# An attention and expert-mixture kernel: expert slots padded to quarters of a tile instead of halves

## Chip, cores and metric

The kernel runs on one core of a Trainium2 chip. The metric is the device time in microseconds (us) of one execution. A core has five engines with queues of their own: TensorE (PE, with its weight loads listed as PEld), VectorE (DVE), ScalarE (ACT), GpSimd (POOL) and SyncE (SP), which here only issues DMAs.

## What is computed

Input x has 2 x 2048 tokens of 256 numbers; all is float32. After a layernorm, two branches are added to x: a linear attention with Chebyshev features and prefix sums, and a mixture of experts in which each token goes to one of 8 experts, beside one shared expert.

```python
xn = _layernorm(x)
# attention: 16 heads of 16, clipped q and k, Chebyshev orders 0..10, cumsum over the tokens
kv_prefix = jnp.cumsum(Tk * v[:, :, :, None, :], axis=2)
ks_prefix = jnp.cumsum(Tk.sum(axis=-1), axis=2)
num = (Tq * kv_prefix * beta).sum(axis=3)
den = (Tq.sum(axis=-1) * ks_prefix * beta).sum(axis=3)
attn = (num / (den + 1e-7)) @ W_out.T
# experts
xf = _layernorm(xn, ln_w, ln_b).reshape(-1, 256)
logits = xf @ router_w
top_idx, top_score = argmax(logits), sigmoid(max(logits))
for e in range(8):                     # g, u: 256 x 512, d: 512 x 256
    xe = xf * where(top_idx == e, top_score, 0.0)
    routed += (silu(xe @ g[e]) * (xe @ u[e])) @ d[e]
shared = (silu(xf @ sh_gate) * (xf @ sh_up)) @ sh_down
out = x + attn + xn + routed + shared
```

## The kernel before

The 4096 tokens are 8 chunks of 512, or 32 tiles of 128. The kernel never runs its stages one after the other. It declares operations (`op`: engine, expected cost, what it reads and writes, a priority, buffers to allocate), and a planner (`Plan.order`) places them on the engines by a model of time: of the operations that are ready, and whose buffers are free, each engine takes the one with the lowest priority number. The planned order is then the program; on the chip each engine runs its own list in that order and waits on semaphores. Priorities put the front first (0), routing (2), scattering (4), expert fetches and small expert work (6), attention (10 and up), the experts' gate and up products (30 and up), and the shared expert last (50 and up), so the shared expert fills PE where nothing else is ready.

**Front.** For each chunk `stat` (L421, L422) takes mean and variance, `roots` (L432 to L456) the inverse roots with one Newton step (L440 to L445; the square root is ACT's, L435), and `front` normalizes (L480, L484), transposes on PE (L505), and evicts to xfT, the experts' input, on ACT (L508) or DVE (L510), and to xnT, the attention's. For chunk 0 the first half of xfT is evicted by ACT, the second by DVE. At the very start ACT issues five small DMAs (L385, L387: ln weights and router) and then runs one square root on a dummy (L390), which loads ACT's table. L462 transposes the ratio that later chunks' xnT need. xnT and most xfT are spilled to DRAM (L566, L571) and loaded again when wanted (L832).

**Routing** (`route`, L675 to L824) is DVE work with two small products: it picks the expert of each token and a slot for it. With padding to whole tiles, 8 experts need up to 39 tiles of 128 slots. The kernel pads to halves: NFULL = 28 tiles hold one expert each, and 15 half tiles (NHALF) follow, two to a tile, so NJ = 36 tiles and NI = 43 sets of expert weights. `odd` counts for each expert the tiles begun, `full` the tiles of which more than a half is used (L711 to L719, a comparison with the multiples of 128, then of 128 plus 64). From them come first and last tile of each expert, the slot of each token (L736 to L762), the expert of each tile (`expert_i`, L768 to L774) and the tables `take_i`, `give_i`, `slot_s` (L781 to L824).

**Experts** (`expert`). For each tile SP reads the expert's number (L1087) and fetches its weights from DRAM, gate and up (L1089) and down (L1095), 512 KiB each, into places of the pool `w_p`. POOL gathers the tokens (L1100); PE transposes them (L1108); ACT scales them (L1111); PE takes the gate and up products (L1118), ACT and DVE silu and product (L1124, L1126), PE transposes (L1131), ACT or DVE copy (L1133, L1134), PE takes the down product (L1139), and after a copy (L1142, L1143) POOL scatters to y_dram (L1146). In a half tile each product is two matmuls with 64 stationary columns each, one for each expert. `w_p` has 8 places of 1024 columns; ten more come from the two attention buffers T when the attention's elementwise work is over. Four of the eight serve the routing tables first.

**Attention** (`attend`): q, k, v products (L907), features on ACT and DVE, prefix sums by scans on DVE (L974), sums over heads on PE (L937, L950, L955: 32 stationary columns each, four groups of columns side by side), denominators (L1018, L1031), output product (L1045).

**Shared expert** (`shared`): gate and up (L845) and down (L862) of each chunk; its xfT, except for chunks 0 to 2, is loaded again into one of four xfT places. A chunk's load waits for the chunk before, and chunks 6 and 7 for the up products of an expert tile near the end (`hold`).

**End**: when all tiles are scattered, y is read back in eight loads (L1169) into xnT and xfT places, added (L1178) and written out (L1182).

The line that sets the order of the tiles before, and the hold:

```python
tiles = sorted(range(NJ), key=lambda j: j if j < NFULL else (j - NFULL + 0.5) * NFULL / n2 - 0.25)
gate, hold = [], {NC - 2: ups[-9], NC - 1: ups[-2]}
```

Of the kernel before, what the change touches and what calls it, by code (L numbers as in the profile page):

```python
# [11 lines left out]
F32 = mybir.dt.float32  # L12
# [24 lines left out]
HF = P // 2  # L37
NFULL = NTT - NE // 2
NHALF = 2 * NTT + NE - 1 - 2 * NFULL
NJ = NFULL + (NHALF + 1) // 2  # L40
NI = NFULL + NHALF
# [214 lines left out]
def kernel(  # L256
# [78 lines left out]
    wide = const.tile([P, 4618], F32, name="wide")  # L335
# [43 lines left out]
    for c in range(NC):  # L379
        if c == 0:  # L380
            for t in range(NT):
# [6 lines left out]
               w=["ln"], nbytes=64 * KiB, prio=-89)  # L388

            op("ACT", 0.2, lambda: A.activation(nu[:, 0, 0:1], ones[:, 0:1], AF.Sqrt), w=["root"], prio=-88.5,  # L390
# [21 lines left out]
    xfTs, xnTs, spilled, fronts, begun = {}, {}, [], [], []  # L412
# [3 lines left out]
    def stat(c):  # L416
        for t in range(NT):
            i = c * NT + t

            def f(c=c, t=t, i=i):  # L420
                V.bn_stats(stats[:, i, :], X[c][:, t, :])  # L421
                V.bn_aggr(mv[:, i, :], stats[:, i, :])  # L422
            op("DVE", 0.58, f, r=[("X", c, t)], w=[("mv", i)], prio=FRONT + 0.1 * c - 0.15)

    def roots(cs):
# [12 lines left out]
        def h():  # L438
# [4 lines left out]
            V.tensor_tensor(u_, u_, v_, ALU.mult)  # L443
            V.tensor_scalar(u_, u_, -0.5, 1.5, ALU.mult, ALU.add)
            V.tensor_tensor(r_, r_, u_, ALU.mult)  # L445
        op("DVE", 1.0, h, r=[("ve", a), ("rs", a)], w=[("r", a // NT + k) for k in range(len(cs))], prio=p)
# [21 lines left out]
    def front(c):  # L468
# [31 lines left out]
        for k in range(KD):  # L500
            bk = Buf(bank_p, f"tr_{c}_{k}")

            def f(bk=bk, k=k):
# [9 lines left out]
            op(*on[k if c == 0 else 0], r=[bk, "ln"], w=[(xfT, k)],  # L513
               prio=p if c else -2.0, alt=on[1:] if c else [])
            if c:
# [117 lines left out]
    def route():  # L633
# [10 lines left out]
        top, idx, lim, pos, tok1, score, hi = (t2(n) for n in ("top", "idx", "lim", "pos", "to", "sc", "hi"))  # L644
# [12 lines left out]

        tile_of = wide[:, : NTT * NJ].rearrange("p (t j) -> p t j", t=NTT)
# [9 lines left out]
        def f():  # L668
# [3 lines left out]
            V.tensor_scalar(lim, iota[:, :NTT], float(P), None, ALU.mult)  # L672
# [33 lines left out]
        def f():  # L706
            for e in range(NE // 2, NE):
                V.tensor_tensor_scan(incl[:, e, :], ones[:, :NTT], tot[:, e, :], 0.0, ALU.mult, ALU.add)

            n_e = incl[:, :, NTT - 1 : NTT].to_broadcast([P, NE, NTT])  # L710
            V.tensor_tensor(gt, n_e, lim.unsqueeze(1).to_broadcast([P, NE, NTT]), ALU.is_gt)  # L711
        op("DVE", 1.3, f, r=["tot", "iota"], w=["gt"], prio=R)

        def f():
            n_e = incl[:, :, NTT - 1 : NTT].to_broadcast([P, NE, NTT])
            V.tensor_reduce(odd, gt, AX.X, ALU.add)
            V.tensor_scalar(lim, lim, float(HF), None, ALU.add)
            V.tensor_tensor(gt, n_e, lim.unsqueeze(1).to_broadcast([P, NE, NTT]), ALU.is_gt)
            V.tensor_reduce(full, gt, AX.X, ALU.add)  # L719
        op("DVE", 1.3, f, r=["gt", "iota"], w=["full"], prio=R)  # L720

        def f():
# [6 lines left out]
            V.tensor_tensor(lft, odd, full, ALU.add)  # L729
            V.scalar_tensor_tensor(lft, wh, -2.0, lft, ALU.mult, ALU.add)  # L730
# [3 lines left out]
        def f():  # L734
# [3 lines left out]
            V.tensor_scalar(lft, lft, float(HF), float(NFULL * P), ALU.mult, ALU.add)  # L738
# [317 lines left out]
    for g in range(KD):  # L1056
# [4 lines left out]
                             zt_p.add([b.t[:, 5120 : 5120 + D]])))  # L1061
    for i, (q, n) in enumerate(((zt_p, D), (sl_p, FF), (hm_p, FF), (yt_p, D))):
# [8 lines left out]
    def expert(n, j):  # L1071
# [3 lines left out]
        if j >= NFULL:  # L1075
            h = NFULL + 2 * (j - NFULL)
            parts = [(h, slice(0, HF)), (h + 1, slice(HF, P))] if h + 1 < NI else [(h, slice(0, P))]
# [7 lines left out]
        for i, ((h, _), (wg, wu, wd)) in enumerate(zip(parts, sets)):  # L1085
            def f(h=h, wg=wg, wu=wu):
                ev.append(nc.values_load(expert_i[0:1, h : h + 1], engines=[SP], min_val=0, max_val=NE - 1))  # L1087
# [137 lines left out]
```

## Time and profile before

| what | value |
|---|---|
| median of 3 runs | 582.14 us (581.93 to 582.86) |
| profiled execution, its own time | 582.48 us |
| its span (first to last instruction) | 580.7 us |
| instructions | 7507 |
| DMA traffic | 110.87 MB, mean 191 GB/s |
| expert gate / up / down loads | 43 each, 512 KiB each |
| L1118 on PE, all forms | 344 instructions listed |
| L1139 on PE, all forms | 344 instructions listed |
| first expert product (L1118) | 139.0 us |
| last load of expert weights issued | 511.69 us |
| last down product (L1139) ends | 544.35 us |
| first y load issued | 548.73 us |
| last matmul ends | 577.06 us |

How to read it: the profile lists for each group of instructions the line of the kernel, engine, operation and shape, the number of instructions, and times in us (means in ns). Each float32 matmul is two matmul instructions on PE. The chain of waits follows what ended last backward to what released it; a row is start, duration, engine and line, and the number of instructions. A stage's row gives start and end, length, busy time of PE, PEld, DVE, ACT and POOL with instruction counts, the granted PE clock, the DMA share and GB/s. The row of a wait gives who waited for whom, the total, how often, and the longest.

### The profile page before, as it was taken

What the parts mean: (1) busy time and instruction counts of PE and PEld (TensorE: products, weight loads), DVE (VectorE), ACT (ScalarE), POOL (GpSimd) and SP (SyncE); (2) the same over time, 40 slices, a digit from 0 to 9 for tenths busy, and PEclk for the clock granted to TensorE, in tenths of its full rate; (3) what the DMA queues carried; (4) which work ended last, traced back from release to release, by engine and by line L of the source; (5) the groups of instructions that cost most, each with busy time, mean ns of one, the idle gap of its engine ahead of it and who ended that gap; (6) DMA issues with size and microseconds to landing.
All of it is one profiled execution on the core that took longest, in us unless ns stands there. A gap on an engine that the chain in (4) does not pass through costs nothing. (4 is left out here: it accounts for less than half of the span.)

```text
span 580.7 us, 7507 instructions
## 1 busy us (share of the span) xinstructions
PE 567.2 (98%) x2439; PEld 312.0 (54%) x2439; DVE 488.4 (84%) x797; ACT 242.6 (42%) x478; POOL 98.5 (17%) x116
## 2 busy tenths in 40 slices
PE   4999999999999999999999999999999999999997
PEld 2446464675554644547464545545465457555565
DVE  6989899999999999999999889999999999433263
ACT  3878872105433553353354454336335432122100
POOL 3201000011211112201303211221121132302100
PEclk9999999999999999999999999999999999999999
DMA  8956570434266825735736672884666386990195
GB/s 270 302 174 215 218 256 34 145 133 126 73 206 216 259 83 175 244 116 165 227 134 209 200 225 70 242 256 156 201 214 199 116 246 228 332 357 28 41 372 176
DMA packets 73142, 110.87 MB, mean 191 GB/s; under 512 B 5425, under 2 KB 44623, under 8 KB 73104
## 3 DMA queue, kind: packets, MB, share of 16 engines
q1 hardware_dynamic: 68144, 99.63, 52.3%
q0 software_dynamic: 4112, 10.77, 5.8%
q8 instruction: 19, 0.31, 0.2%
q10 hardware_dynamic: 848, 0.01, 0.1%
q14 instruction: 19, 0.16, 0.1%
HBM read 91.50 MB, written 19.41 MB: 191 GB/s over the span
## 5 line engine op out<-in xcount | busy, mean ns | idle before, releaser
L1118 PE MATMUL bank<-big,wide 128*128 128x512 f32 (+1 forms) x320 | 122.3, 599 | 0.0
L1146 POOL DMA_INDIRECT y_dram<-wide,give_i x34 | 42.5, 1249 | 308.2 <-ACT wide L1142 159.3
L907 PE MATMUL bank<-xnT,w_in 128*128 128x512 f32 x192 | 87.4, 595 | 0.0
L974 DVE TENSOR_TENSOR_SCAN tv<-ones,carry,tv 128x512 f32<-128x512 f32 x60 | 76.6, 1276 | 1.1
L1118 PEld LDWEIGHTS bank<-big,wide 128*128 128x128 f32 (+1 forms) x320 | 44.7, 171 | 56.4 <-issue 54.5
L845 PE MATMUL bank<-xfT,sg 128*128 128x512 f32 x128 | 62.4, 610 | 0.1
L1139 PE MATMUL bank<-big,wide 128*128 128x256 f32 (+1 forms) x312 | 61.8, 386 | 0.0
L845 PE MATMUL bank<-xfT,su 128*128 128x512 f32 x128 | 60.7, 597 | 0.0
L862 PE MATMUL bank<-sd,hT 128*128 128x256 f32 x256 | 57.6, 380 | 0.0
L907 PEld LDWEIGHTS bank<-xnT,w_in 128*128 128x128 f32 x192 | 35.4, 190 | 38.1 <-issue 34.1
L1139 PEld LDWEIGHTS bank<-big,wide 128*128 128x128 f32 (+1 forms) x312 | 44.0, 171 | 20.5 <-issue 9.7
L862 PEld LDWEIGHTS bank<-sd,hT 128*128 128x128 f32 x256 | 48.0, 190 | 10.0 <-issue 3.0
L1100 POOL DMA_INDIRECT wide<-z_dram,take_i x33 | 38.4, 1163 | 78.5 <-DVE wide L823 68.7
L851 ACT ACTIVATE hT<-bank 128x512 f32<-128x512 f32 x32 | 19.1, 596 | 75.7 <-PE bank L845 74.9
L1124 ACT ACTIVATE wide<-bank,slot_s 128x512 f32<-128x512 f32 x35 | 24.1, 687 | 61.1 <-PE bank L1118 61.1
L994 DVE TENSOR_TENSOR o<-o,tv 128x512 f32<-128x512 f32 x64 | 44.2, 691 | 1.7
L1126 DVE SCALAR_TENSOR_TENSOR wide<-bank,slot_s,wide 128x512 f32<-128x512 f32 x35 | 26.2, 748 | 19.0 <-PE bank L1118 17.1
L1111 ACT ACTIVATE wide<-bank,lnb,lnw 128x128 f32<-128x128 f32 x72 | 29.1, 457 | 25.0 <-PE bank L1108 25.0
L929 DVE SCALAR_TENSOR_TENSOR T<-T 128x1024 f32<-128x1024 f32 x32 | 38.3, 1216 | 0.0
L845 PEld LDWEIGHTS bank<-xfT,sg 128*128 128x128 f32 x128 | 23.5, 194 | 26.8 <-issue 23.3
L845 PEld LDWEIGHTS bank<-xfT,su 128*128 128x128 f32 x128 | 23.2, 190 | 25.5 <-issue 24.5
L853 DVE TENSOR_TENSOR hT<-hT,bank 128x512 f32<-128x512 f32 x32 | 21.9, 684 | 16.1 <-PE bank L845 15.0
(209 smaller groups left out, 804.7 us busy)
## 6 DMA issues: line engine op xcount, KB each, us to landing
big<-in_gate_w SPq DMA_DIRECT2D x40, 512.0 KB
big<-in_up_w SPq DMA_DIRECT2D x40, 512.0 KB
big<-in_down_w SPq DMA_DIRECT2D x39, 512.0 KB
z_dram<-big SPq DMA_DIRECT2D x8, 512.0 KB
X<-in_x SPq DMA_DIRECT2D x7, 512.0 KB
xn_dram<-xnT SPq DMA_DIRECT2D x7, 512.0 KB
xnT<-xn_dram SPq DMA_DIRECT2D x7, 512.0 KB
out<-X SPq DMA_DIRECT2D x7, 512.0 KB
```

The lines of the kernel that those rows point to most:

```text
L845: T_.matmul(b.t, wt[:, k, ts(f, P)], vx(k), start=(k == 0), stop=(k == KD - 1))
L862: T_.matmul(po.t[:, ts(i, D)], hT[f].t[:, ts(tp * 2 + i, P)], sd[:, f, :], start=(f == 0), stop=(f == KF - 1))
L907: T_.matmul(pm.t, w_in[:, k, ds(i * D + g * P, P)], xnT.t[:, ts(k, CH)], start=(k == 0), stop=(k == KD - 1))
L929: op("DVE", 1.27, lambda i=i, j=j, q=part: V.scalar_tensor_tensor(q[i](), q[j](), off[i], q[1](), ALU.subtract, ALU.mult), r=[(T, j)] + X2 ...
L974: o_ = op("DVE", 1.25, lambda b=b, i=i, g=g: V.tensor_tensor_scan(b.t, ones[:, 0:1].to_broadcast([P, CH]), b.t, 0.0 if opening else old[:, ...
L994: op("DVE", 0.66, lambda o=o, b=b: V.tensor_tensor(o(), o(), b.t, ALU.add), r=[b, ok], w=[ok], prio=p)
L1100: op("POOL", 1.28, lambda: G.indirect_dma_start(out=zt.t, out_offset=None, in_=z_dram, in_offset=bass.IndirectOffsetOnAxis(ap=take_i[:, j ...
L1111: op("ACT", 0.46, lambda k=k: A.activation(xT.t[:, ts(k, P)], pz.t[:, ts(k, P)], AF.Identity, bias=lnb[:, k : k + 1], scale=lnw[:, k : k + ...
L1118: T_.matmul(b.t[n, :], xT.t[:, ds(k * P + n.start, n.stop - n.start)], wt.t[:, ts(k, FF)], start=(k == 0), stop=(k == KD - 1), skip_group_ ...
L1126: op("DVE", 0.75, lambda: V.scalar_tensor_tensor(sl.t, pu.t, sc(), sl.t, ALU.mult, ALU.mult), r=[pu, zt, sl], w=[sl], prio=EXQ)
L1139: T_.matmul(py.t[n, :D], hmT.t[:, ds(i * P + n.start, n.stop - n.start)], wd.t[:, ts(i, D)], start=(i == 0), stop=(i == KF - 1), skip_grou ...
L1146: y_ins.append(G.indirect_dma_start(out=y_dram, out_offset=bass.IndirectOffsetOnAxis(ap=give_i[:, j : j + 1], axis=0), in_=yt.t, in_offset ...
```

## The change

- Slots are padded to quarters of a tile (32 slots). NFULL = 26 tiles of one expert, NPART = 31 quarters, four to a tile, in 8 more tiles (the last has three): NJ = 34 tiles, NI = 57 weight sets. A mixed tile has an expert in each quarter of its columns, so each of its products is four matmuls with 32 stationary columns.
- Routing counts quarters: one comparison of each expert's count with 128 multiples of 32 (`over`, in memory that the ratio rows used, hence its wait on the last xn_dram write), one sum for `odd` (quarters begun) and one over every fourth for `full`.
- The weights are fetched one at a time: all gates of a tile, then all ups, then all downs, each fetch with its own place.
- Two of the four xfT places go to `w_p` when the front's spills are issued (`V_`).
- The mixed tiles come first and then after each 3.7 whole tiles or so (before: after each 3.5); chunks 6 and 7 of the shared expert wait for the 14th and 4th last up products (before: 9th and 2nd).
- At the start: ACT's dummy square root comes ahead of its DMAs; the statistics of later chunks wait until chunk 0's second eviction has been issued (`evicted`); the Newton step has four DVE operations instead of five.

```diff
-HF = P // 2
-NFULL = NTT - NE // 2
-NHALF = 2 * NTT + NE - 1 - 2 * NFULL
-NJ = NFULL + (NHALF + 1) // 2
-NI = NFULL + NHALF
+NFULL = NTT - 3 * NE // 4
+NPART = 4 * NTT + NE - 1 - 4 * NFULL
+NJ = NFULL + (NPART + 3) // 4
+NI = NFULL + NPART
...
-               w=["ln"], nbytes=64 * KiB, prio=-89)
-            op("ACT", 0.2, lambda: A.activation(nu[:, 0, 0:1], ones[:, 0:1], AF.Sqrt), w=["root"], prio=-88.5,
+               w=["ln"], nbytes=64 * KiB, prio=-88.5)
+            op("ACT", 0.2, lambda: A.activation(nu[:, 0, 0:1], ones[:, 0:1], AF.Sqrt), w=["root"], prio=-89,
...
-            op("DVE", 0.58, f, r=[("X", c, t)], w=[("mv", i)], prio=FRONT + 0.1 * c - 0.15)
+            op("DVE", 0.58, f, r=[("X", c, t)], w=[("mv", i)], prio=FRONT + 0.1 * c - 0.15, after=evicted)
...
-            V.tensor_tensor(u_, u_, v_, ALU.mult)
-            V.tensor_scalar(u_, u_, -0.5, 1.5, ALU.mult, ALU.add)
-            V.tensor_tensor(r_, r_, u_, ALU.mult)
+            V.scalar_tensor_tensor(u_, u_, -0.5, v_, ALU.mult, ALU.mult)
+            V.scalar_tensor_tensor(r_, u_, 1.5, r_, ALU.add, ALU.mult)
...
-            op(*on[k if c == 0 else 0], r=[bk, "ln"], w=[(xfT, k)],
+            o = op(*on[k if c == 0 else 0], r=[bk, "ln"], w=[(xfT, k)],
                prio=p if c else -2.0, alt=on[1:] if c else [])
+            if c == 0:
+                evicted[:] = [o]
...
-            n_e = incl[:, :, NTT - 1 : NTT].to_broadcast([P, NE, NTT])
-            V.tensor_tensor(gt, n_e, lim.unsqueeze(1).to_broadcast([P, NE, NTT]), ALU.is_gt)
...
-            V.tensor_reduce(odd, gt, AX.X, ALU.add)
-            V.tensor_scalar(lim, lim, float(HF), None, ALU.add)
-            V.tensor_tensor(gt, n_e, lim.unsqueeze(1).to_broadcast([P, NE, NTT]), ALU.is_gt)
-            V.tensor_reduce(full, gt, AX.X, ALU.add)
+            V.tensor_tensor(
+                over, incl[:, :, NTT - 1 : NTT].to_broadcast([P, NE, 4 * NTT]),
+                quart.unsqueeze(1).to_broadcast([P, NE, 4 * NTT]), ALU.is_gt,
+            )
+        op("DVE", 1.3, f, r=["incl", "iota", ("xn_dram", NC - 1)], w=["gt"], prio=R)
...
+            V.tensor_reduce(odd, over, AX.X, ALU.add)
+            V.tensor_reduce(full, over.rearrange("p e (t q) -> p e t q", q=4)[:, :, :, 3], AX.X, ALU.add)
...
-            V.tensor_tensor(lft, odd, full, ALU.add)
-            V.scalar_tensor_tensor(lft, wh, -2.0, lft, ALU.mult, ALU.add)
+            V.scalar_tensor_tensor(lft, wh, -4.0, odd, ALU.mult, ALU.add)
...
+    for i in range(2):
+        b = Buf(xfT_p, f"V_{i}")
+        b.users = 1
+        op("SP", 0.01, lambda: None, alloc=[b], prio=ROUTE, after=list(spilled),
+           grow=lambda b=b: w_p.add([b.t]))
...
-            h = NFULL + 2 * (j - NFULL)
-            parts = [(h, slice(0, HF)), (h + 1, slice(HF, P))] if h + 1 < NI else [(h, slice(0, P))]
+            h = NFULL + 4 * (j - NFULL)
+            m = min(4, NI - h)
+            parts = [(h + i, slice(i * QD, (i + 1) * QD if i < m - 1 else P)) for i in range(m)]
...
-            fetch = op("SP", 1.3, f, r=["experts"] + [("z_dram", n) for n in range(NC)], w=[wg, wu], alloc=[wg, wu],
-                       nbytes=KiB * KiB, prio=EXQ + e, after=downs[-1:])
...
+        for n, src, cost in ((0, gate_w, 0.85), (1, up_w, 0.45), (2, down_w, 0.45)):
+            for i, (h, _) in enumerate(parts):
+                def f(h=h, i=i, n=n, src=src, b=sets[i][n]):
+                    if n == 0:
+                        ev.append(nc.values_load(expert_i[0:1, h : h + 1], engines=[SP], min_val=0, max_val=NE - 1))
+                    S_.dma_start(out=b.t.rearrange("p (k f) -> p k f", k=KF if n == 2 else KD),
+                                 in_=src[ds(ev[i], 1)].rearrange("o (k p) f -> p (o k) f", p=P))
+                downs.append(op("SP", cost, f, r=["experts"] + [("z_dram", n) for n in range(NC)], w=[sets[i][n]],
+                                alloc=[sets[i][n]], nbytes=512 * KiB, prio=EXQ + e, after=downs[-1:]))
...
-    tiles = sorted(range(NJ), key=lambda j: j if j < NFULL else (j - NFULL + 0.5) * NFULL / n2 - 0.25)
+    tiles = sorted(range(NJ), key=lambda j: j if j < NFULL else 3.7 * (j - NFULL) - 0.5)
...
-    gate, hold = [], {NC - 2: ups[-9], NC - 1: ups[-2]}
+    gate, hold = [], {NC - 2: ups[-14], NC - 1: ups[-4]}
```

## The prediction

> **What bounds the kernel now.** I read the busy times and the 40 slices first:
>
> ```profile
> PE 567.2 (98%) x2439; PEld 312.0 (54%) x2439; DVE 488.4 (84%) x797; ACT 242.6 (42%) x478; POOL 98.5 (17%) x116
> PE   4999999999999999999999999999999999999997
> DVE  6989899999999999999999889999999999433263
> ```
>
> TensorE works from 8.21 us (its first matmul) to 577.06 us (its last). Its clock was granted at full in every slice, so time is saved only by giving PE less work, or lost by making it wait. Second, DVE is 9 in nearly every slice until about 493 us, where the last attention chunk's elementwise work ends; after that it is half idle. PE therefore fills the gaps of a DVE-paced attention with expert tiles, and what is left with the shared expert.
>
> Then the chain of waits, which from 320 us on is almost only PE; its rows give the price of each kind of PE work:
>
> ```profile
> 355.01 0.86 PE psq L937 x8
> 357.79 1.00 PE psk L937 x8
> ...
> 443.37 1.87 PE bank L1118 x8
> ...
> 489.61 1.73 PE bank L1139 x8
> ...
> 504.38 1.88 PE bank L1139 x16
> ...
> 511.60 0.22 PE bank L1108 x2
> 511.82 0.44 PE bank L1131 x4
> 512.26 1.72 PE bank L1118 x4
> ```
>
> L1118 with 4 instructions is the gate (or up) product of a whole tile; with 8, of a half tile (two experts, 64 columns each): 1.87 against 1.72. So two column halves run side by side, at 0.15 for the change of form. L937 is the same with 32 columns, four groups side by side: 8 instructions of 512 elements take 0.86, or 1.00 where the form is entered. That is the shape the quarter tiles will have.
>
> Last the waits of the SP queue and two stages at the end:
>
> ```profile
> SPq L1089 <- PE bank L1139: 95.3, 20, 13.5
> SPq L1089 <- PE bank L1118: 56.3, 27, 10.8
> SPq L1095 <- PE bank L1118: 54.9, 19, 12.5
> ...
> 490.00:512.00 22.00, 22.00 (x91) 11.69 (x90) 11.22 (x19) 4.79 (x12) 6.55 (x6) 1.00 0.90 295
> 512.00:548.00 36.00, 36.00 (x130) 21.89 (x129) 11.13 (x18) 7.45 (x16) 5.93 (x6) 1.00 0.33 118
> ```
>
> SP, which fetches the experts' weights, mostly waits for PE to give a weight buffer back: buffers, not bandwidth, hold the fetch. From 140 to 490 us the DMA share is 0.59 at 186 GB/s; in the dense part after 497 us slices reach 350 to 425 GB/s, about 375, so one 512 KiB load costs 0.524 MB / 375 = 1.4 us at best.
>
> **The change, part by part.**
>
> *Two tiles fewer.* NJ goes from 36 to 34. A whole tile on PE is 0.22 + 1.72 + 1.72 + 0.44 + 1.73 = 5.83; two are **-11.7 us**, all on the engine that sets the end.
>
> *Quarters for halves.* Seven half tiles paid 0.15 three times (gate, up, down): 7 x 0.45 = 3.2. Eight quarter tiles, if L937 is the pattern, pay 0.14 to 0.15 three times: 8 x 0.45 = 3.6. I take **+0.5**. For the down product (four groups that move 256 elements) there is no row. The low bound is the same price; the high bound comes from L1018 (32 columns, 128 elements), whose 8 instructions take 0.36, 0.18 a wave of four where half of 0.215 (an eighth of 1.72) would be 0.11: 0.07 x 8 waves x 8 tiles = +4.5. L1118's and L937's forms are nearer in length, so I stay at the low end.
>
> Here a rule of the Trainium skill speaks against the change. The row first: L937's four groups took 0.86 to 1.00 where one full-width product takes 0.86, so 3.4 to 4 times one group's work. "TensorE: Matmul & The Clock Gate", section "Measured speedup vs the span model", gives three column tiles of 32 as 2.38 times, 79% of ideal. By that, as an estimate, the 5.17 us of products in a quarter tile become 6.5, eight tiles cost +11, and the saving is gone: about 581. The measured row decides, and I do not use the page's figure.
>
> *Weights.* Each quarter tile fetches four experts: 57 sets instead of 43, or 171 loads instead of 129, +22 MB; SP issues 42 more at 0.37 us each, which its long waits hide. At 1.4 us a load, 171 loads are 240 of the 430 us between 107 us (first fetch) and the last tile, so bandwidth is enough. What decides is the buffers. Before: 8 loads issued by 140 us, 104 between 140 and 490, 17 after; with 8 buffers one load stays in its buffer for 350 x 8 / 104 = 27 us. After: 10 buffers (two freed xfT places join). To be as far at 490 us as before, 171 x 112 / 129 = 148 loads must be out; less the 10 of the first fill, 138 in 350 us, so a stay of 25.4 us. This is 6% less than 27. Gate, up and down are now fetched singly, gates of all four experts first, which helps: before, gate and up were planned as a pair that needed two free buffers at once. The cover for a late weight is shared-expert work: of its 165 us (256 L845 instructions at 0.43, 256 L862 at 0.215), some 42 us were spent between 140 and 490 as filler (56 and 80 instructions in the trace), and the new holds (the 14th and 4th last tile instead of the 9th and 2nd) release chunks 6 and 7 earlier. If the stay remains 27 us: 350 x 10 / 27 + 10 = 140 loads by 490, 31 left, 31 x 1.4 = 43 us, last weights at 533 and, with some 8 us for the last tile, last expert product at 541. Before it was 544.35. So even an unchanged stay is just good enough. I take 1.5 us for extra PE waits at quarter tiles (before: PE's waits after the start came to 1.5 in all) with bounds 0 and 15.
>
> *After the last expert tile.* Two xfT places fewer mean three y loads in flight at the end, where five were issued between 548.73 and 551.4. A load takes 552.64 - 548.73 = 3.9 and its addition 1.22, so three buffers pass eight chunks in about 14 us; the additions in the trace are spread to 570.85 anyhow, behind PE. Nothing, as long as the shared filler (33 us of PE after 544.35) covers it; without that cover this tail of some 30 us (8.4 MB at 375 GB/s is 22.4, plus 4.4 from the last product to the first y load, plus latency and last addition) ends the kernel by itself.
>
> *Routing.* Removed: L711, L716, L717, L718, L719 (0.43 + 0.42 + 0.17 + 0.43 + 0.42 = 1.87) and L729 (0.17). Added: a comparison and a sum over 1024 elements, 1.2 each by L781 (1184 elements, 1.37) and L788 (1152, 1.35), a sum over 256 at 0.42, and about 0.25 for 57 instead of 43 experts in L768 and L772. Table work shrinks by 36 to 34 columns: -0.4. Net about +0.6 us of DVE. It lies before 127 us, while PE has shared work (L845 runs back to back from 96 to 106); behind it queue the first gather and expert tile at 138.9. The added wait for xn_dram's last write costs nothing: it was issued at 79.3, the comparison runs at about 94. I take 0, bounds 0 and +0.6.
>
> *The start.* The rows, of ACT, DVE and PE in order of time:
>
> ```profile
> 4.98 1.28 ACT L390 ACT_TABLE_LOAD   x1 [4.98 <-DMA lnw<-in_ln_w]
> 6.38 0.19 ACT L435 ACTIVATE rs<-ve 128x8 f32<-128x8 f32 x1
> 10.46 3.94 PE L845 MATMUL bank<-xfT,sg 128*128 128x512 f32 x4
> 11.72 0.81 DVE L510 TENSOR_SCALAR xfT<-bank,lnw,lnb 128x512 f32<-128x512 f32 x1
> ```
>
> The square root's table now loads before ACT's five DMA issues. The variances are ready at 5.82, so the root starts 0.5 earlier; one DVE operation fewer saves 0.2. The second eviction (L510) moves ahead of chunk 1's four statistics, and PE's second pair of L845 no longer stands for 2 us. But L462 waits for chunk 1's ratio at 16.58, which comes only 0.5 to 0.7 earlier, so most of the 2 us is handed on to that wait. The moved DMAs (lnw, lnb, router) are issued some 1.5 us later; lnw took 2.65 to land, so about 5 us, and is first used at 9.65: covered. Past that cover SP suffers: L392, and behind it sg, su and chunk 1, waited for such a landing (3.48). If it does again, chunk 1 is 1.5 later. I take **-0.8**, bounds -2 and +1.
>
> *Sum*, against the profiled execution's own 582.48 (span 580.7, 1.8 around it): 582.48 - 11.7 + 0.5 + 1.5 - 0.8 = 572.0. The median of the runs shown is 0.34 lower, which is inside the working: **572**.
>
> **Rivals.**
>
> *The tail shows (still faster).* Weights come a little late, PE spends the shared filler before the last expert tile, and the tail of 30 to 33 us ends the kernel. By the sums above with a last product between 544 and 548: span 575 to 580, so 576 to 581. For it: the final stage has 18 buffers' worth of loads and the quarter tiles reach into it (the last one is the last tile). Against: chunks 6 and 7 can be held for the tail by the plan.
>
> *Slower: the buffers.* One mechanism: a quarter tile needs 4 gates at once and 12 loads in all through 10 buffers, and the stay grows. At 30 us only 350 x 10 / 30 + 10 = 127 loads are out by 490; 44 left, 62 us, last product at 560, plus 32: span 592, **594**. It decides from a stay of 28 us: 135 loads out, 36 left, 50 us, last product at 548.7, plus 32 is the old 580.7. For it: loads per tile grow by 5.03 / 3.58 = 1.40 and buffers by 1.25, and a half tile's first gate already lay 40 us (fetched at 193.56, used at 229.56, released after 233). Against: PE's only waits for data now are 1.5 us, and much of a stay is PE doing attention.
>
> *Not what it says.* The four groups run one after the other: three more times 5.17 us, eight times, +124: 696. L937 is against it.
>
> **How the numbers follow.** Forecast 0.45 (own range 568 to 575.5), visible tail 0.24, within no change 0.05, slower by buffers 0.25, serial groups 0.01. No change means within 0.2%, 581.0 to 583.3, about what a measurement of this kernel can tell. So faster 0.69, same 0.05, slower 0.26. The predicted time is the likeliest case's. The range 567 to 588 takes in the start's and the down product's bounds, the tail and half of the slower case.
>
> **What would show it.** Right: PE busy near 556 us and still 9 in every slice; L1118 of the 32-column form at 16 instructions in some 1.9 us; PE's waits for weights under 3 us; last expert product before 541. Wrong: PE rows waiting for gate weights, or a PE that ends 5 us or more before the span does; L1139 of 32 columns above 2.2 us a tile; L505 at the start not before 8 us. Weights that lie 28 us or longer in the buffers would make the forecast wrong at its root.

## The result, and the profile after

The changed kernel takes **591.49 us** (median of 4 runs, 589.52 to 591.74) against 582.26 (median of 4, 581.93 to 582.86): a ratio of 1.015, 95% interval 1.0127 to 1.0173. It is slower by 9.2 us, where 572 was forecast. The profiled execution took 589.52 us, with a span of 587.6. Line numbers from here on are those of the changed kernel unless a run of the kernel before is meant: L504 is the front's transpose (before L505), L849 and L866 the shared expert (L845, L862), L911 the attention's q, k, v (L907), L1107 the gather (L1100), L1115 its transpose (L1108), L1125 gate and up (L1118), L1146 down (L1139), L1153 the scatter (L1146).

First the page of the changed kernel, busy times and slices:

```profile
PE 561.6 (96%) x2651; PEld 303.1 (52%) x2651; DVE 484.2 (82%) x784; ACT 242.4 (41%) x474; POOL 97.5 (17%) x112
PE   1999999999999999899899998999999999999997
DVE  3889999999999999899979988999989998831253
```

PE's busy time has fallen by 5.6 us, half of what was expected, and its line now has holes: a 1 in the first slice (before a 4), and eights between 235 and 367 us. DVE's line dips in the same stretch, so it has not taken over as the bound. The span grew although the work shrank, so the loss is in waiting. The waits of PE (who waited for whom, total, times, longest) name the place:

```profile
PE bank L504 <- DVE big L479: 13.0, 1, 13.0
PE bank L1115 <- DMA wide<-z_dram,take_i: 8.2, 7, 2.8
PE bank L911 <- ACT wide L1140: 0.7, 1, 0.7
```

The kernel before had these:

```profile
PE bank L505 <- DVE big L480: 8.2, 1, 8.2
PE bank L1108 <- DMA wide<-z_dram,take_i: 1.3, 1, 1.3
```

No row of the changed kernel has a weight's load in it. Two rows have grown: the first matmul, and the transposes of gathered tokens, 1.3 us before and 8.2 now.

**The start.** ACT's rows in order of time (start, duration, engine, line, operation, and in brackets the idle time before it):

```profile
0.82 1.28 ACT L389 ACT_TABLE_LOAD   x1 [0.82 <-PEq L1218]
2.11 0.20 ACT L389 ACTIVATE nu<-ones 128x1 f32<-128x1 f32 x1
2.99 0.41 ACTq L384 DMA_DIRECT2D lnw<-in_ln_w  x1
3.96 0.33 ACTq L384 DMA_DIRECT2D lnb<-in_ln_b  x1
4.51 0.33 ACTq L384 DMA_DIRECT2D lnw<-in_ln_w  x1
6.80 0.33 ACTq L384 DMA_DIRECT2D lnb<-in_ln_b  x1
10.89 0.39 ACTq L386 DMA_DIRECT2D rw<-in_router_w  x1
11.32 0.21 ACT L435 ACTIVATE rs<-ve 128x8 f32<-128x8 f32 x1 [9.01 <-DMA lnw<-in_ln_w]
```

The last two of the five small DMAs before, and two of SP's loads in the changed kernel:

```profile
2.23 0.46 ACTq L385 DMA_DIRECT2D lnb<-in_ln_b  x1
4.56 0.39 ACTq L387 DMA_DIRECT2D rw<-in_router_w  x1
```

```profile
2.68 0.43 SPq L391 DMA_DIRECT2D sg<-in_sh_gate  x1
...
3.67 0.47 SPq L396 DMA_DIRECT2D X<-in_x  x1
```

The table is loaded at 2.1 us, as meant. But the five small DMAs, of which the first four had gone by 2.7 us before, now go at 2.99, 3.96, 4.51, 6.80 and 10.89, and the root that the first transposes need (L435) stands behind them on ACT: 11.32 instead of 6.38. Each row of a DMA in the trace carries the semaphore that it raises. SP's and ACT's DMAs use the same eight, 100 to 107, and take them in turn by planned order; one that is given a semaphore already in use has a wait on it. Before, ACT's four norm loads were among the first eight and waited for nothing. Now SP has taken all eight: the second lnb load waits on 104, which the shared expert's 512 KiB gate load raises (landed at 6.78; the lnb load goes at 6.80), and the router's load waits on 106, for the 512 KiB load of chunk 1 issued at 3.67 (landed at 10.81; the router's load goes at 10.89). PE's first matmul moves from 8.21 to 12.97.

**The middle.** The stage from 140 to 490 us, with length, busy PE, PEld, DVE, ACT and POOL, granted clock, DMA share and GB/s:

```profile
140.00:490.00 350.00, 340.98 (x1741) 175.15 (x1740) 319.89 (x422) 155.13 (x317) 68.62 (x54) 1.00 0.72 241
```

PE is idle for 9.0 of the 350 us. A gather (L1107) writes into one of four places. In the planner's model a place comes free only when the tile that had it, four tiles earlier, has been scattered (L1153), so in POOL's list the gather stands behind that scatter. POOL's rows around the longest wait show that chain:

```profile
280.18 1.38 POOL L1153 DMA_INDIRECT y_dram<-wide,give_i  x1 [11.61 <-ACT wide L1149]
285.12 1.51 POOL L1153 DMA_INDIRECT y_dram<-wide,give_i  x1 [3.56 <-ACT carry L984]
286.94 1.04 POOL L1107 DMA_INDIRECT wide<-z_dram,take_i  x1 [0.30 <-issue]
288.29 1.02 POOL L1107 DMA_INDIRECT wide<-z_dram,take_i  x1 [0.30 <-issue]
```

Two scatters stand ahead of two gathers, the gathers follow at once, and PE's transpose (L1115) waits until 294.39 for a gather issued at 286.94 or 288.29. From issue to landing a gather takes 5.2 us in the median (5.4 before): the transfer is no slower, it starts too late.

**The end.** In the chain of waits (start, duration, what) the expert products of mixed tiles appear with their price:

```profile
486.22 1.85 PE bank L1125 x16
...
493.35 1.86 PE bank L1146 x32
...
527.09 3.97 PE bank L1125 x12
...
532.99 3.97 PE bank L1125 x12
...
542.74 4.53 PE bank L1146 x24
547.27 10.50 PE bank L849 x24
```

Four quarters side by side take 1.85 for a product, as forecast. The last mixed tile has only three experts, and the third has the last 64 columns (the slice ends at P): 12 instructions instead of 16, and 3.97 and 4.53 us instead of 1.85.

The weights: the last load is issued at 512.2 (before 511.7), 10 loads by 140 us and 154 by 490, so one stays 350 x 10 / 144 = 24.3 us in its buffer. The last expert product ends at 547.27, and PE has 36 us of shared work after it.

### The profile page after: what moved, and what is told of

Read it like the earlier page. It is cut to its first block, busy times and chain, and to the rows that moved or that the text cites. A ratio compares the mean times of both kernels' runs of the same rounds, so it can differ in the third digit from the quotient of the medians.

```text
span 587.6 us, 8097 instructions
## 1 busy us (share of the span) xinstructions
PE 561.6 (96%) x2651; PEld 303.1 (52%) x2651; DVE 484.2 (82%) x784; ACT 242.4 (41%) x474; POOL 97.5 (17%) x112
## 5 line engine op out<-in xcount | busy, mean ns | idle before, releaser
L1125 PE MATMUL bank<-big,wide 128*32 128x512 f32 (+1 forms) x356 | 109.0, 599 | 0.0
L1153 POOL DMA_INDIRECT y_dram<-wide,give_i x33 | 41.7, 1262 | 316.9 <-ACT wide L1149 222.3
L911 PE MATMUL bank<-xnT,w_in 128*128 128x512 f32 x192 | 87.5, 595 | 0.7 <-ACT wide L1140 0.7
L849 PE MATMUL bank<-xfT,sg 128*128 128x512 f32 x128 | 61.8, 605 | 0.0
L849 PE MATMUL bank<-xfT,su 128*128 128x512 f32 x128 | 60.4, 594 | 0.0
L1125 PEld LDWEIGHTS bank<-big,wide 128*32 128x32 f32 (+1 forms) x356 | 36.8, 148 | 43.1 <-issue 42.3
L866 PE MATMUL bank<-sd,hT 128*128 128x256 f32 x256 | 57.7, 380 | 0.0
L911 PEld LDWEIGHTS bank<-xnT,w_in 128*128 128x128 f32 x192 | 35.1, 190 | 38.1 <-issue 35.1
L1107 POOL DMA_INDIRECT wide<-z_dram,take_i x33 | 40.7, 1233 | 80.0 <-DVE give_i L828 70.2
L866 PEld LDWEIGHTS bank<-sd,hT 128*128 128x128 f32 x256 | 48.0, 190 | 10.4 <-issue 4.0
L1146 PE MATMUL bank<-big,wide 128*32 128x256 f32 (+1 forms) x328 | 51.3, 383 | 0.0
L1131 ACT ACTIVATE wide<-bank,slot_s 128x512 f32<-128x512 f32 x33 | 22.7, 689 | 53.6 <-PE bank L1125 50.8
L1146 PEld LDWEIGHTS bank<-big,wide 128*32 128x32 f32 (+1 forms) x328 | 36.1, 149 | 14.6 <-issue 3.0
L857 DVE TENSOR_TENSOR hT<-hT,bank 128x512 f32<-128x512 f32 x32 | 21.8, 682 | 19.9 <-PE bank L849 19.6
L849 PEld LDWEIGHTS bank<-xfT,sg 128*128 128x128 f32 x128 | 23.1, 193 | 27.6 <-issue 22.8
L849 PEld LDWEIGHTS bank<-xfT,su 128*128 128x128 f32 x128 | 23.6, 190 | 26.0 <-issue 25.0
L919 ACT ACTIVATE T<-bank 128x512 f32<-128x512 f32 x32 | 19.1, 598 | 41.6 <-PE bank L911 38.2
L1133 DVE SCALAR_TENSOR_TENSOR wide<-bank,slot_s,wide 128x512 f32<-128x512 f32 x33 | 24.6, 746 | 14.1 <-PE bank L1125 12.2
```

Source lines behind the costliest of these rows:

```text
L849: T_.matmul(b.t, wt[:, k, ts(f, P)], vx(k), start=(k == 0), stop=(k == KD - 1))
L866: T_.matmul(po.t[:, ts(i, D)], hT[f].t[:, ts(tp * 2 + i, P)], sd[:, f, :], start=(f == 0), stop=(f == KF - 1))
L911: T_.matmul(pm.t, w_in[:, k, ds(i * D + g * P, P)], xnT.t[:, ts(k, CH)], start=(k == 0), stop=(k == KD - 1))
L1107: op("POOL", 1.28, lambda: G.indirect_dma_start(out=zt.t, out_offset=None, in_=z_dram, in_offset=bass.IndirectOffsetOnAxis(ap=take_i[:, j ...
L1125: T_.matmul(b.t[n, :], xT.t[:, ds(k * P + n.start, n.stop - n.start)], wt.t[:, ts(k, FF)], start=(k == 0), stop=(k == KD - 1), skip_group_ ...
L1131: op("ACT", 0.7, lambda: A.activation(sl.t, pg.t, AF.Silu, scale=sc()), r=[pg, zt], w=[sl], alloc=[sl], prio=EXQ, table="silu")
```

## The experiments

Each was timed beside the kernel before on the same chip; that kernel's medians there were 582.43 (e1, e2, e3, e5), 582.08 (e6 to e9), 582.69 (e10, e14) and 583.52 (e15). First matmul and gather waits are those of one profiled execution, in us.

| run | median us | ratio to before, 95% interval | first matmul | gather waits of PE |
|---|---|---|---|---|
| changed kernel | 591.49 | 1.015 (1.0127 to 1.0173) | 12.97 | 8.2 |
| e1_start | 588.74 | 1.0104 (1.0055 to 1.0154) | 8.1 | 8.3 |
| e2_last | 584.93 | 1.0045 (1.0015 to 1.0075) | 13.2 | 5.7 |
| e3_zt | 583.18 | 1.0014 (0.9996 to 1.0031) | 13.6 | none |
| e15_early_alone | 578.84 | 0.9919 (0.989 to 0.9948) | 13.3 | none |
| e5_all | 571.40 | 0.9799 (0.9764 to 0.9834) | 8.0 | none |
| e8_w8 | 582.18 | 1.0008 (0.9987 to 1.0029) | 8.1 | none |
| e9_early | 567.22 | 0.9745 (0.9709 to 0.978) | 8.0 | none |
| e10_early_split | 566.60 | 0.9705 (0.9663 to 0.9747) | 7.6 | none |
| e6_before_act | 587.08 | 1.0104 (1.0058 to 1.015) | 13.5 | 1.1 |
| e7_before_evict | 583.19 | 1.0022 (1.0005 to 1.0039) | 8.1 | 2.0 |
| e14_before_early | 580.18 | 0.9951 (0.9932 to 0.997) | 8.3 | none |

### ACT's order at the start: e1_start and e6_before_act

In the changed kernel the old order is put back; in the kernel before, only this part of the change is made.

```diff
 # e1_start, on the changed kernel (e6_before_act is the reverse, on the kernel before)
-               w=["ln"], nbytes=64 * KiB, prio=-88.5)
+               w=["ln"], nbytes=64 * KiB, prio=-89)
...
-            op("ACT", 0.2, lambda: A.activation(nu[:, 0, 0:1], ones[:, 0:1], AF.Sqrt), w=["root"], prio=-89,
+            op("ACT", 0.2, lambda: A.activation(nu[:, 0, 0:1], ones[:, 0:1], AF.Sqrt), w=["root"], prio=-88.5,
```

> The changed kernel with ACT's five small DMAs ahead of the dummy square root again, as before; PE's, DVE's, POOL's and SP's orders are those of the changed kernel. Theory (in the changed kernel ACT's DMAs each wait for the landing of the DMA that used their semaphore last, the fifth until 10.8 us, and the first real square root stands behind them): that root starts near 6.4 instead of 11.32, the first matmul near 8.0 instead of 12.97, and the whole order moves 4 to 5 us earlier: 591.5 becomes 586.5 to 587.5. Rival (the start does not matter, since PE waits later for gathered tokens or weights anyway): above 590, with PE's waits in the middle grown by what was won at the start.

> The kernel before with one edit of the change: ACT's dummy square root ahead of its five DMAs. The orders of PE and SP stay as before. Theory (the DMAs then stand behind the landings of larger ones, and the first real root behind them): first matmul near 13 instead of 8.2, and since PE has no slack later, 582.4 + 4.7 = 587, between 586 and 588. Rival (only the changed kernel's order pays for a late start): under 583.5.

In the kernel before, the reordering alone costs 5.0 us (587.08 against 582.08). Its waits show that little else has moved:

```profile
PE bank L505 <- DVE big L480: 13.5, 1, 13.5
PE bank L1108 <- DMA wide<-z_dram,take_i: 1.1, 2, 0.9
```

The first matmul stands 13.5 us instead of 8.2, and those 5.3 are the loss. In the changed kernel, putting the order back brings the first matmul to 8.1, but the time falls by only 2.75, less than the theory and more than the rival. The rest is seen in the profiles. PE's 2651 matmul instructions have the same order in both. At the first one e1_start is 4.9 us ahead; 1.4 of it is gone within 10 us. The first products of the shared expert, in e1_start and then in the changed kernel:

```profile
10.33 3.78 PE L849 MATMUL bank<-xfT,sg 128*128 128x512 f32 x4
```

```profile
15.22 2.68 PE L849 MATMUL bank<-xfT,sg 128*128 128x512 f32 x4
```

Another 1.7 go in the rows that follow e1_start's longest wait for a gather; the line below them is the stage of the four slow matmuls, with the granted clock third from its end:

```profile
290.89 0.44 PE L1115 MATMUL bank<-ident,wide 128*128 128x128 f32 x2 [2.66 <-DMA wide<-z_dram,take_i]
291.14 3.58 PE L911 MATMUL bank<-xnT,w_in 128*128 128x512 f32 x4
```

```profile
291.14:294.50 3.36, 3.36 (x6) 1.34 (x5) 1.39 (x2) 0.89 (x3) 0.00 (x0) 0.50 0.00 0
```

The same place in the changed kernel's own profile:

```profile
294.39 0.41 PE L1115 MATMUL bank<-ident,wide 128*128 128x128 f32 x2 [2.75 <-DMA wide<-z_dram,take_i]
294.64 1.88 PE L911 MATMUL bank<-xnT,w_in 128*128 128x512 f32 x4
```

Four matmuls of 512 elements take 3.58 in the one, at a granted clock of 0.50, and 1.88 in the other, after waits of nearly the same length. So a wait of this kind can cost another 1.7 us of half-speed work, in some executions and not in others. With 1.4 and 1.7 of the 4.9 gone, the two profiled spans differ by 2.0 (587.6 and 585.6). e1_start has two executions, with a granted clock of 0.996 and 0.993 over the whole span (the changed kernel's four: 0.997 to 0.999), so the price of the late start in the changed kernel, between 2.75 and the 5.0 of e6_before_act, stays uncertain.

### The last mixed tile: e2_last

Its third expert takes two quarters of 32 columns instead of one slice of 64; the weights are the same.

```diff
+        runs = [(min(i, len(parts) - 1), slice(i * QD, (i + 1) * QD)) for i in range(4)] if j >= NFULL else [(0, slice(0, P))]
...
-                for (_, n), wt in zip(parts, wts_):
+                for n, wt in [(n, wts_[i]) for i, n in runs]:
...
-                for (_, n), wd in zip(parts, wds):
+                for n, wd in [(n, wds[i]) for i, n in runs]:
```

> The changed kernel with the last mixed tile in four quarters of 32 columns, its third expert in the last two, instead of 32, 32 and 64; every other engine's order is the same. Theory (a 64-column product does not run beside 32-column ones, and each change of form costs): gate and up of that tile take 1.75 to 1.85 each instead of 3.97, down 1.85 instead of 4.53, the last matmul ends 7 us earlier: 584 to 585. Rival (the read-back of y and the output, not PE, set the end): PE ends earlier but the time falls by less than 2.

The time is 584.93 (580.57 to 588.68), 6.6 less than the changed kernel's. With so wide a spread the rows are the better witness. The chain of waits shows the same tile with 16, 16 and 32 instructions:

```profile
525.04 1.85 PE bank L1125 x16
...
528.82 1.85 PE bank L1125 x16
...
536.46 1.86 PE bank L1146 x32
```

From 3.97 + 3.97 + 4.53 to 1.85 + 1.85 + 1.86: 6.9 us, by doing more instructions. In the changed kernel's trace the gate product goes in four stretches:

```profile
527.02 1.05 PE L1125 MATMUL bank<-big,wide 128*32 128x512 f32 x4
528.00 1.07 PE L1125 MATMUL bank<-T,wide 128*64 128x512 f32 x2
529.01 1.05 PE L1125 MATMUL bank<-big,wide 128*32 128x512 f32 x4
529.99 1.07 PE L1125 MATMUL bank<-T,wide 128*64 128x512 f32 x2
```

By their starts, and the next product's at 530.99, the two narrow groups run beside each other, the wide one beside neither: each stretch takes 0.98 to 1.01, where two instructions of one form alone take 0.86. That is 4 x 0.86 = 3.44 for work one behind the other, and 0.53 for four changes of form, 0.13 each; a product of four quarters pays the same 0.13 once (1.85 against 1.72). The Trainium skill, "TensorEngine Tiling (Array Packing)", section "Key Properties", says that changing the tiling mode, as against the tile, drains TensorE. These rows agree with it.

### The gathers' places: e3_zt, e15_early_alone and e14_before_early

e3_zt gives one of the two freed xfT places to the gathers: four more places, and nine weight buffers instead of ten. e15_early_alone leaves the ten and shortens what a place is held for: silu, product and scatter no longer name the gathered tile among the things that they read (they never use it), so in the planner's model its place is free once it is transposed. e14_before_early is the same edit in the kernel before.

```diff
 # e3_zt
-           grow=lambda b=b: w_p.add([b.t]))
+           grow=lambda b=b, i=i: zt_p.add([b.t[:, k * D : (k + 1) * D] for k in range(4)]) if i else w_p.add([b.t]))
 # e15_early_alone, e14_before_early
-        op("ACT", 0.7, ... r=[pg, zt], w=[sl]
+        op("ACT", 0.7, ... r=[pg], w=[sl]
-           r=[pu, zt, sl], w=[sl], prio=EXQ)
+           r=[pu, sl], w=[sl], prio=EXQ)
-        op("POOL", 1.28, f, r=[yt, zt, "table"], w=[("y", j)]
+        op("POOL", 1.28, f, r=[yt, "table"], w=[("y", j)]
```

> The changed kernel with the second freed xfT place cut into four more places for gathered tokens, and so 9 instead of 10 weight buffers until the attention ends; the plan's order changes with it. Theory (PE's 8 to 10 us of waits in the middle come from four places for gathered tokens: a gather can start only when the scatter four tiles back is done): PE's waits for gathers fall under 2 us; the time falls by 6 to 8, to 583.5 to 585.5. Rival (weight buffers are what is short): with one buffer less PE waits for weights, the last expert product is later than 547, and the time is 591 or more.

> The changed kernel with one edit: a gathered tile's place is free once the tile is transposed. All else stays, the ten weight buffers too. Theory (the changed kernel loses 8.2 us of PE time to gathers that wait for one of four places, and another 1 to 2 us to half-speed matmuls after these waits): PE waits for gathers under 1.5 us, 581.5 to 583.5. Rival (what the run with four more places won came from its other order, or PE's time goes to weights once the gathers come early): PE's waits for weights above 3 us and 586 or more.

> The kernel before, in halves, with the one edit that a gathered tile's place is free once it is transposed. Theory (before waits only 1.3 us for gathers, so there is little to win; what the four repairs together gain comes from the quarters): 580.5 to 582.5, ratio 0.997 to 1.001, and the quarters net 13 to 15 us against it. Rival (the early release of places is worth as much to the halves, by an order that the planner finds better): 575 or less.

e3_zt took 583.18, 8.3 less. e15_early_alone took 578.84, 12.7 less (13.5 by the two ratios to the kernel before, which was slower on this chip), more than the 581.5 to 583.5 of the theory, and its waits have one row left, the start's:

```profile
PE bank L504 <- DVE big L479: 13.3, 1, 13.3
```

From the issue of a gather to the start of its tile's transposes lie 40.5 us on average over the tiles, where the changed kernel has 12.2. The starts of the matmuls in the changed kernel's trace show eight gaps between 238 and 486 us, 10.2 us in all (the 8.2 of the table of waits, what it puts down to ACT, and a rest); none of them is left here, and the two spans differ by 10.8. The medians differ by 1.9 more, which fits half-speed matmuls after such waits but is not shown: all eight runs here had a granted clock of 1.0, and the changed kernel's slower three had 0.997 to 0.999. That e3_zt gained 4.3 less, with one weight buffer fewer, was not followed further.

In the halves the same edit gains 2.5 (580.18 against 582.69), a little more than the theory allowed: the kernel before waited for gathers only once. So the early release is not all that separates halves from quarters.

### The repairs together: e5_all and e9_early

> The three edits together: ACT's order of before, the last mixed tile in four quarters, four more places for gathered tokens. Theory (three causes that add): 591.5 - 4.8 - 7 - 7 = 572.7, between 570 and 576, faster than the kernel before by 1 to 2%. Rival (the causes hide one another, or the tail of read-back and output then ends the kernel): 578 or more.

> Old ACT order and four quarters in the last tile; the gathered tokens still have four places, but a place is counted free when the tile is transposed, no longer only when the tile is scattered; the weights keep ten buffers. Theory (a gather is late because its place is held until the scatter four tiles back): PE's waits for gathers fall under 1.5, time 570 to 573.5. Rival (gathers are late because they run slowly beside more weight traffic, or because POOL issues them behind scatters): the waits stay at 5 or more and the time is 576 or more.

With the first three edits (e5_all) the time is 571.40, 1.3 below the expectation. With the early release in place of the extra places (e9_early) it is 567.22, 4.2 lower again and below the range given: the ten weight buffers are kept, 167 loads are out by 490 us instead of 159, and the last expert product ends at 514.7 instead of 529.8. PE's only wait after the start is 0.9 us for one weight. With the start's price from e6_before_act the single prices add up: 591.49 - 5.0 - 6.6 (last tile) - 12.7 (gathers) = 567.2. With the 2.75 that e1_start gained the sum is 569.4, so the close agreement is partly luck.

### Fewer weight buffers: e8_w8

With start and last tile repaired, both freed xfT places go to the gathers, and eight weight buffers remain.

```diff
-           grow=lambda b=b: w_p.add([b.t]))
+           grow=lambda b=b, i=i: zt_p.add([b.t[:, k * D : (k + 1) * D] for k in range(4)]))
```

> The three edits (old ACT order, four quarters in the last tile, more places for gathered tokens), but both freed xfT places go to gathered tokens, so the weights have 8 buffers as before the change while the attention runs. Theory (weights have slack, the prediction's slower rival was wrong): within 2.5 of the version with nine, 569 to 574, PE's waits for weights under 3. Rival (weight buffers are short; the prediction's sum with a stay of 27 us: 112 loads by 490, 59 left at 1.4 us): 590 or more.

582.18: neither the theory (within 2.5 us of e5_all) nor the rival (590 and more). No weight makes PE wait, and yet 141 loads are out by 490 us, the last goes at 529.9 instead of 502.4, and the last expert product ends at 548.2 instead of 529.8. PE's slices, and the end of the chain of waits:

```profile
PE   4999999999999999999999999999999999999892
```

```profile
548.16 10.51 PE bank L849 x24
...
561.09 5.30 DMA xfT<-y_dram
...
568.14 6.81 DMA xfT<-y_dram
...
575.04 1.23 DVE X L1184
```

PE runs out of work at 569.0, before the span does, and the read-back of y ends the kernel, 580.5 - 548.2 = 32.3 us after the last expert product. The first 10.5 of these in the chain are still shared work, behind whose elementwise product on DVE (L857) an addition of y stands. Against e5_all this is one weight buffer fewer, eight for nine, and four more places for gathers: 10.8 us more. With ten, in e9_early, it is 15.0 us.

### The other start edits: e7_before_evict

The kernel before with the statistics behind the second eviction and the shorter Newton step, as in the change.

> The kernel before with the other two edits of the start: statistics of later chunks behind chunk 0's second eviction, and the Newton step in four DVE operations. Theory (the prediction's: 2 us of PE's standing are handed on to the wait for chunk 1's ratio, 0.5 to 0.7 earlier): 0.3 to 1 us faster, 581.4 to 582.1. Rivals: all of the 2 us is won, 580.4; or the order that the planner makes of it is worse, above 582.6.

DVE's rows show the eviction first, at 10.35, where it stood at 11.72 before:

```profile
10.35 0.81 DVE L509 TENSOR_SCALAR xfT<-bank,lnw,lnb 128x512 f32<-128x512 f32 x1 [1.21 <-PE bank L504]
```

And yet the time is 583.19, 1.1 above the kernel before (1.0005 to 1.0039), as the last rival had it. The gain is handed back later; the profiled execution has 3.2 us of waits after the start where the kernel before had 1.5, in a new planned order:

```profile
PE bank L1109 <- DMA wide<-z_dram,take_i: 2.0, 2, 1.4
PE bank L1132 <- DVE wide L1127: 1.2, 2, 0.9
```

### The router's load behind the table: e10_early_split

e9_early with the router's load as an operation of its own, behind the dummy root; the first router product names it as read.

```diff
-            ] + [A.dma_start(out=rw[:, :, :NE], in_=router_w.rearrange("(k p) e -> p k e", p=P))],
-               w=["ln"], nbytes=64 * KiB, prio=-89)
+            ], w=["ln"], nbytes=4 * KiB, prio=-89)
+            op("ACT", 0.45, lambda: A.dma_start(out=rw[:, :, :NE], in_=router_w.rearrange("(k p) e -> p k e", p=P)), w=["rw"], nbytes=64 * KiB, prio=-88.2)
...
```

> The kernel with all three repairs of the changed one (ACT's start order of before, the last mixed tile in four 32-column quarters, a gathered tile's place free once it is transposed), and in it the load of the router's weights put behind the dummy root instead of between the norm's loads. Theory (a small load behind others on ACT waits until the semaphore that it is given has seen its earlier transfer land): the dummy root then goes about 0.5 us earlier (some 5.8 us instead of 6.4), the router's weights come in time for the first router product, and the time falls by 0.3 to 0.7 us, to about 566.7. Rival (the router's load then waits for its semaphore and holds the root of the variances behind it): first matmul not earlier than 8.0 us, or later; time 567 to 570.

566.60, 0.6 less by the medians, in the expected range; the two were timed on different chips and their times touch (566.12 to 566.83, and 566.49 to 569.01), so the rows say more. The first matmul is 0.4 earlier, and ACT's rows show why:

```profile
2.71 1.28 ACT L389 ACT_TABLE_LOAD   x1 [2.71 <-issue]
...
4.57 0.43 ACTq L387 DMA_DIRECT2D rw<-in_router_w  x1
5.94 0.21 ACT L435 ACTIVATE rs<-ve 128x8 f32<-128x8 f32 x1 [1.73 <-DVE ve L433]
```

The table loads in the 2 us in which the router's DMA waits for its semaphore anyhow, and the root now waits for the variances: it has nothing more to gain from ACT. This is what the reordering of the change was after, and it is the fastest of the versions: 2.95% under the kernel before (2.53 to 3.37), with PE at 98% of its span.

## Why the prediction was wrong

- **Two tiles fewer, -11.7, and quarter forms, +0.5: right, and a little better.** Taking out the gaps between the starts of matmuls, PE's work is 564.8 us before and 551.9 in e10_early_split, 12.9 less where 11.2 was forecast. A product of four quarters took 1.74 to 1.86, the low end of the bounds; the high end for the down product (+4.5) did not come, nor did groups one after the other. The figure of 2.38 in the Trainium skill for three column tiles ("TensorE: Matmul & The Clock Gate", "Measured speedup vs the span model") would have made it, as an estimate from that page, about 2.2 us a product (1.72 x 3 / 2.38). The measured rows decide against it here. (The prediction's "about 581" for that case should, by its own terms, be 582.5.) Against e14_before_early, the best of the halves, e9_early is 13.0 us faster by the medians and 12.0 by the two ratios, with the gathers' release and ACT's order alike. The other edits of the start, the order of the tiles, the holds, the single fetches and two more weight buffers differ too, and no run takes those apart, but for e7_before_evict.
- **The quarter tiles' count of columns: the step that was missing.** Eight tiles were costed as "four experts each"; the diff's `QD if i < m - 1 else P` makes the last one 32, 32 and 64. That tile cost 6.6 us (e2_last), more than half of the two saved tiles.
- **The start, -0.8 with bounds -2 and +1: wrong in sign and size.** It measured +4.8 at the first matmul and +5.0 in time (e6_before_act); taking it back in the changed kernel gained 2.75. "The moved DMAs ... are issued some 1.5 us later ... covered" failed: they were issued up to 6.3 us later (the router's, 4.56 to 10.89), because each waits for the landing of a larger transfer on the same semaphore, and nothing covered the root behind them on ACT. That SP could suffer from such waits was said; that ACT could was not. The rest of the term failed too: the other two edits, alone on the kernel before, cost 1.1 us (e7_before_evict). And the 2 us for which PE's second pair of L845 was said to stand were at most in part a wait for the eviction: with the eviction ahead, the same four matmuls, 3.94 before, still took between 2.68 (the changed kernel) and 3.78 (e1_start).
- **Weights and buffers, waits +1.5: right for weights, wrong for what was left out.** No weight made PE wait, and the stay was 24.3 us where 25.4 was needed. But the gathers have only four places, held until the scatter, and the prediction did not look at them. The loss was 10.2 us of PE in the profiled execution, and 12.7 by e15_early_alone. It lies within the bound of 15 given for waits of another kind, which is no merit of the step. Gathers were late in the old order already: from a gather's issue to the start of its tile's transposes it was 13.2 us on average over the tiles before, 12.2 after. Why this makes PE wait seven times in the new order and once in the old, the runs do not settle.
- **After the last expert tile, 0: right as it stands.** 36 us of shared work followed the last product. The tail's length, 30 to 33 us, came out at 32.3 in e8_w8, though with 10.5 us of shared work still in its chain. There the rival "the tail shows" came true by its mechanism; in the changed kernel it did not.
- **Slower by buffers, 594 (0.25): near in time and wrong in mechanism.** With ten buffers the stay never came near 28 us. With eight, in e8_w8, it is 350 x 8 / 133 = 21 us; the loads are late there because there are fewer buffers, not because each is held longer on average.
- **Routing, 0: not tested by itself.** No wait of PE after the start and before the first tile stands in the tables.

Of the signs named: the 16-instruction rows and the waits for weights came right; PE's 556 (561.6) with a 9 in every slice, the last product before 541 (547.3) and the start before 8 us (12.97) came wrong, and the start was the one named as a way to be wrong.

The sum, mended with what was measured: 582.48 - 11.7 + 0.5 + 4.8 + 6.6 + 10.2 = 592.9, against 589.5 in the profiled execution. PE's work fell by 1.7 more than forecast, and the 10.2 stand against 1.9 of the same gaps before; with both the sum is 589.3. This is closer than the terms are: in the profiled execution 1.3 of the start's 4.8 came back at once (the first four matmuls of the shared expert took 2.68 where the kernel before had 3.94), which the sum leaves out, and the last tile cost 6.9 by its rows.

## What to carry to other kernels

Read a diff's edge cases as tiles of their own: one mixed tile out of eight, of another form, cost more than half of what two saved tiles brought. Before a small DMA is moved on a queue, look at which landing it will wait for in its new place and what stands behind it on that engine. When a change raises the load on one pool of buffers, count the places of every pool that the same tiles pass through, and until when each is held; here a shorter hold (12.7 us) was worth more than four more places at the price of a weight buffer (8.3).

## What the runs showed of the hardware that was not expected

- In the last mixed tile, matmuls with 64 stationary columns did not run beside ones with 32: 3.97 us for 12 instructions, 1.85 for 16 of one form.
- After PE waits of 2.66 and 2.75 us the next four 512-element matmuls took 3.58 us in one execution, at a granted clock of 0.50, and 1.88 in another, at 1.00. The Trainium skill, "TensorE: Matmul & The Clock Gate", "Part 1: The HAM clock gate", says that the array falls to half its clock after an idle window of some 3.4 us, that the window runs free and that the effect differs from run to run. Here a wait shorter than that window was enough, in one of the two.
- DMAs of different engines waited for each other without sharing a queue, data or a buffer, because the program gives them the same semaphores: the second lnb load, 128 numbers on ACT, stood until 6.80 us for a 512 KiB load that SP had issued at 2.68, and the router's load until 10.89 for one issued at 3.67.
